# Expert rows scattered to their tokens' places by each block, and read back in order

## The chip, the cores and the metric

The kernel runs on one core of a Trainium2 chip. The metric is the device time of one execution in microseconds. The program in question has three timed runs: 1660.15, 1660.92 and 1669.7 us, with a median of 1660.92. Beside them one execution was recorded by the profiler.

## The reference, cut to what matters

A graph transformer layer over 1250 tokens of width 768 in float32. Two branches (graph attention over 20000 edges, and linear attention) are added to x; then comes a mixture of experts with a shared expert. Only this last part bears on the change:

```python
probs = softmax(x @ router_w)                      # 8 experts
gates, idx = top_k(probs, 2)
gates = gates / sum(gates)
g = silu(einsum('bsd,edh->bseh', x, w_gate))       # each w: [8, 768, 768]
u = einsum('bsd,edh->bseh', x, w_up)
expert_out = einsum('bseh,ehd->bsed', g * u, w_down)
routed = sum over the two chosen experts of gate * expert_out
shared = silu(x @ ws_gate) * (x @ ws_up) @ ws_down # width 384
alpha = sigmoid(x @ sg_w + sg_b)
out = x + alpha * shared + (1 - alpha) * routed
```

In the layer `x` enters this part normalised. Only the two chosen experts of a token have to be computed: 2500 rows of work.

## The kernel before

Tokens are tiled by 125 (`TP`), ten tiles (`NT`). The residual `acc`, 125 x 10 x 768, stays in SBUF for the whole kernel. The program is built with a scheduler that orders each engine's instructions by priority and puts in the waits; a queue (SP, ACT or POOL) issues its DMAs strictly in its own order, each after the semaphores it waits for.

The expert part sorts rows by expert. Each token's two rows get a slot number (`slot`). An expert's slots are rounded up to parts of 64 rows, and two parts make a block of 128 slots. There may be up to 26 blocks (`NBLK`); 22 of them (`NSURE`) run unconditionally, and the last four stand under nested conditions on the number of parts in use (`n_part`).

Five steps matter here.

- **Routing.** Normalised tokens go to DRAM (`xd`, L765). Twenty indirect DMAs on POOL, the puts (L836), write each token's number to `who` at its slot. `who` was zeroed at the start of the kernel, so an unused slot names token 0. SP loads `who` back as `ids` (L842), one column for each block. Meanwhile TensorE computes the shared expert's hidden rows (L880).
- **Inputs of a block.** `gather` (L908) fetches the block's 128 token rows by an indirect DMA on POOL. `fetch` (L915) loads one of the three expert matrices of the block (2304 KB) on SP, into a ring of two places. Since a block can take its first part's weights from either place, a place is loaded again only when the block before has finished with its product.
- **The block.** `rows` transposes the inputs, `gate` and `up` make the hidden rows, `hidden` transposes them, `down` makes the output rows. The loop overlaps `down` of one block with the next block's products. After `down`, VectorE copies the result out of PSUM (L969) and ACT stores it to `ys` in slot order (L970), one plain DMA of 128 x 768.
- **Ahead.** The loop also fetches weights, and gathers rows, for block 22, which stands under a condition; inside the conditions each block does so for the next one.
- **The end.** For each token tile, two indirect DMAs on POOL gather the 125 rows of its two choices from `ys` into `yg` (L1026). For each tile in turn, TensorE multiplies the shared hidden rows by `wsd` (L1034), VectorE adds the shared part (L1037) and the two routed parts (L1039) to `acc`, and the tile is stored, 120 rows by SP (L1042) and 5 by ACT (L1043).

The blocks that do not run leave their `ys` rows unwritten, so four stores of zeros fill them early (L328).

Of the kernel before, what the change touches and what calls it, by code (L numbers as in the profile page):

```python
# [8 lines left out]
F32 = mybir.dt.float32  # L9
# [4 lines left out]
I32 = mybir.dt.int32  # L14
AF = mybir.ActivationFunctionType
ALU = mybir.AluOpType
# [3 lines left out]
P = 128  # L20
TP = 125
NT = 10
N = TP * NT
D = 768
# [21 lines left out]
NBLK = -(-((NE - 2) * NPART - 2 * (-N // PART)) // NPART)  # L46
NSURE = -(-(2 * N + NE * PART // 2) // P)
NSLOT = NBLK * P
# [14 lines left out]
def gps_block(ctx: ExitStack, tc: tile.TileContext, x, src, dst, norm_g, norm_b, W1, a_src1, a_dst1, b1,  # L63
              W2, a_src2, a_dst2, b2, Wu, bu, w_qkv, w_proj, b_proj, router_w, w_gate, w_up, w_down,
              ws_gate, ws_up, ws_down, sg_w, sg_b, out):
    nc = tc.nc
# [2 lines left out]
    big = ctx.enter_context(tc.tile_pool(name="big", bufs=1, reuse_waits="tile"))  # L69
    dram = ctx.enter_context(tc.tile_pool(name="slots", bufs=1, space=bass.MemoryType.DRAM))  # L70

    xd = dram.tile([N, D], F32, name="xd")
    who = dram.tile([NSLOT, 1], I32, name="who")
    ys = dram.tile([NSLOT, D], F32, name="ys")
    xd_t = xd.rearrange("(t p) d -> t p d", p=TP)
    who_b = who.rearrange("(b p) o -> b (p o)", p=P)
    who_p = who.rearrange("(b p) o -> p (b o)", p=P)
    ys_b = ys.rearrange("(b p) d -> b p d", p=P)


    acc = big.tile([TP, NT, D], F32, name="acc")
# [81 lines left out]
    with tc.tile_pool(name="ph1", bufs=1, reuse_waits="tile") as p1, tc.tile_pool(name="ph1w", bufs=2, reuse_waits="tile") as p1w, \  # L163
# [55 lines left out]
        for j in range(2):  # L219
            o = H2 * (C2 + 1) + j * H2  # L220
# [11 lines left out]
        for k in range(KD):  # L232
# [10 lines left out]
            for h in range(H1):  # L243
                o = (h % 2) * CG
# [8 lines left out]
        for h in range(H1):  # L253
            o = (h % 2) * CG
# [20 lines left out]
        for h in range(H2):  # L275
            o = h * (C2 + 1) + C2
# [23 lines left out]
        base = p1.tile([TP, ECH], F32, name="base")  # L300
# [19 lines left out]
    with tc.tile_pool(name="cnt", bufs=1, reuse_waits="tile") as cp, \  # L320
            tc.tile_pool(name="tokps", bufs=2, space=PSUM, reuse_waits="tile") as ps, \
            tc.tile_pool(name="cntps", bufs=3, space=PSUM, reuse_waits="tile") as pcp:

        zero = cp.tile([P, D], F32, name="zero")
        nc.gpsimd.memset(zero, 0.0)
        nc.sync.dma_start(who_b, zero[:NBLK, :P].bitcast(I32))
        for j in range(NSURE, NBLK):
            nc.sync.dma_start(ys_b[j], zero)  # L328

# [66 lines left out]
        for t0 in range(0, NT, 2):  # L398
            ts = range(t0, t0 + 2)
            mv, r, r2 = ahead  # L400
# [210 lines left out]
    with tc.tile_pool(name="h2p", bufs=1, reuse_waits="tile") as hp, tc.tile_pool(name="gatw", bufs=2, reuse_waits="tile") as pw:  # L611
# [23 lines left out]
        with tc.tile_pool(name="wup", bufs=1, side="right", reuse_waits="tile") as wp2, \  # L635
# [53 lines left out]
            o = H2 * (C2 + 1)  # L689
# [19 lines left out]
    fp = ctx.enter_context(tc.tile_pool(name="ffn", bufs=1, reuse_waits="tile"))  # L709

    g2 = fp.tile([TP, NT, 2], F32, name="g2")
    al = fp.tile([TP, NT], F32, name="al")
    slot = fp.tile([TP, 2, NT], I32, name="slot")
    blk = fp.tile([TP, NBLK + 1], I32, name="blk")
    place = fp.tile([TP, NBLK, NPART], I32, name="place")
    ids = fp.tile([P, NBLK], I32, name="ids")
    nh = HS // P
    hTs_s = fp.tile([P, nh, N], F32, name="hTs_s")
    wsd = fp.tile([P, nh, D], F32, name="wsd")
# [13 lines left out]
    with tc.tile_pool(name="fln", bufs=2, reuse_waits="tile") as pw, tc.tile_pool(name="flnps", bufs=1, space=PSUM, reuse_waits="tile") as ps:  # L733
# [8 lines left out]
                                base=0, pattern=[[1, TP]], channel_multiplier=-1)  # L742
# [9 lines left out]
        rev = pw.tile([TP, NT, NE], F32, name="rev", bufs=1)  # L752
        nc.gpsimd.iota(rev, pattern=[[0, NT], [-1, NE]], base=NE, channel_multiplier=0,
                       allow_small_or_imprecise_dtypes=True)
        number = pw.tile([TP, NT], I32, name="number", bufs=1)
        nc.gpsimd.iota(number, pattern=[[TP, NT]], base=0, channel_multiplier=1)
        norms = []
        for t0, n in ((0, 2), (2, 4), (6, 4)):
            mv, r = moments(pw, [acc[:, t, :] for t in range(t0, t0 + n)], f"ln3_{t0}")
# [28 lines left out]
        for r in range(2):  # L788
            m = pw.tile([TP, NT], F32, name=f"r_m{r}", bufs=1)
            nc.vector.tensor_reduce(m, pb, axis=AX.X, op=ALU.max)  # L790
            o = pw.tile(S3, F32, name=f"r_o{r}", bufs=1)
            nc.vector.tensor_tensor(o, pb, m[:, :, None].to_broadcast(S3), ALU.is_equal)
            nc.vector.tensor_mul(o, o, rev)
            f = pw.tile([TP, NT], F32, name=f"r_f{r}", bufs=1)
# [25 lines left out]
        for e in range(NE):  # L820
# [3 lines left out]
                                       op0=ALU.mult, op1=ALU.add)  # L824
# [9 lines left out]
        for t in range(NT):  # L834
            for r in range(2):
                put = nc.gpsimd.indirect_dma_start(  # L836
                    out=who, out_offset=bass.IndirectOffsetOnAxis(ap=slot[:, r, t:t + 1], axis=0),
                    in_=number[:, t:t + 1], in_offset=None, bounds_check=NSLOT - 1, oob_is_err=False)
                for p in puts:
                    tc.declare_no_dep(put.ins, p.ins, reason="slots differ")  # L840
                puts.append(put)
# [49 lines left out]
    with tc.tile_pool(name="fps", bufs=1, space=PSUM, reuse_waits="tile") as ps:  # L891
# [4 lines left out]
        xin = [xpool.tile([P, D], F32, name=f"xin{i}") for i in two]  # L896
# [9 lines left out]
        experts, spots = {}, {}  # L906

        def gather(j):  # L908
            if j < NBLK:
                nc.gpsimd.indirect_dma_start(  # L910
                    out=xin[j % 2], out_offset=None, in_=xd,
                    in_offset=bass.IndirectOffsetOnAxis(ap=ids[:, j:j + 1], axis=0),
                    bounds_check=N - 1, oob_is_err=False)

        def fetch(j, i):  # L915

            if j >= NBLK:
                return
            if i == 0:
                experts[j] = nc.sync.value_load(blk[0:1, j:j + 1], min_val=0, max_val=NE - 1)  # L920
            w = (w_gate, w_up, w_down)[i]
            nc.sync.dma_start(rings[i][:, j % 2], w[bass.ds(experts[j], 1)].rearrange("o (k p) f -> p (o k) f", p=P))

        def places(j):

            at = [j % 2] * NPART
            if j > 0:
                for i in range(NPART - 1):
                    at[i] = nc.tensor.value_load(place[0:1, j, i:i + 1], min_val=0, max_val=1)
            spots[j] = at  # L930
# [20 lines left out]
        def hidden(j):  # L951
            turned(hTs[j % 2], hs[j % 2])

        def gate(j, s):
            h = hs[j % 2][:, s * HALF:(s + 1) * HALF]
            product(j, 0, pgs[s], xTs[j % 2], s)
            nc.scalar.activation(h, pgs[s][:, :HALF], AF.Sigmoid)  # L957
            nc.vector.tensor_mul(h, h, pgs[s][:, :HALF])  # L958
# [6 lines left out]
        def down(j):  # L965
            y = yo[j % 2]
            for s in two:
                product(j, 2, pd[:, s], hTs[j % 2], s)
            nc.vector.tensor_copy(y.rearrange("p (s d) -> p s d", s=2), pd[:, :, :HALF])  # L969
            nc.scalar.dma_start(ys_b[j], y)  # L970


        for j in two:
            gather(j)
            for i in range(2):
                fetch(j, i)
            if j == 0:
                fetch(j, 2)
        places(0)
        rows(0)  # L980
        for j in range(NSURE):
            gate(j, 0)
            if j > 0:
                hidden(j - 1)
            gate(j, 1)
            if j > 0 and j + 1 < NSURE + 1:
                fetch(j + 1, 0)
            if j + 1 < NSURE:
                places(j + 1)
            for s in two:  # L990
                up(j, s)
            if j > 0 and j + 1 < NSURE + 1:
                fetch(j + 1, 1)
            gather(j + 2) if j + 2 < NSURE + 1 else None
            if j + 1 < NSURE:
                rows(j + 1)
            if j > 0:
                down(j - 1)
                fetch(j, 2)
        hidden(NSURE - 1)  # L1000
        down(NSURE - 1)
        fetch(NSURE, 2)

        with ExitStack() as deeper:
            for j in range(NSURE, NBLK):
                deeper.enter_context(tc.If(n_part > j * NPART))
                gather(j + 1)
                places(j)
                rows(j)
                for s in two:  # L1010
                    gate(j, s)
                fetch(j + 1, 0)
                for s in two:
                    up(j, s)
                fetch(j + 1, 1)
                hidden(j)
                down(j)
                fetch(j + 1, 2)
    blocks.close()

    out_t = out.rearrange("(t p) d -> p t d", p=TP)
    with tc.tile_pool(name="comb", bufs=1, reuse_waits="tile") as cb, tc.tile_pool(name="cps", bufs=3, space=PSUM, reuse_waits="tile") as ps:
        ygs = [cb.tile([TP, D], F32, name=f"yg{i}") for i in range(2 * NT)]
        for t in range(NT):
            for r in range(2):
                nc.gpsimd.indirect_dma_start(  # L1026
                    out=ygs[2 * t + r], out_offset=None, in_=ys,
                    in_offset=bass.IndirectOffsetOnAxis(ap=slot[:, r, t:t + 1], axis=0),
                    bounds_check=NSLOT - 1, oob_is_err=False)
        for t in range(NT):  # L1030
            pd = ps.tile([TP, 2, 512], F32, name="pds")
            for s in range(2):
                for f in range(nh):
                    nc.tensor.matmul(pd[:, s, :HALF], hTs_s[:, f, t * TP:(t + 1) * TP],  # L1034
                                     wsd[:, f, s * HALF:(s + 1) * HALF], start=(f == 0), stop=(f == nh - 1))
            av = acc[:, t, :].rearrange("p (s d) -> p s d", s=2)
            nc.vector.scalar_tensor_tensor(av, pd[:, :, :HALF], al[:, t:t + 1], av, op0=ALU.mult, op1=ALU.add)  # L1037
            for r in range(2):
                nc.vector.scalar_tensor_tensor(acc[:, t, :], ygs[2 * t + r], g2[:, t, r:r + 1], acc[:, t, :],  # L1039
                                               op0=ALU.mult, op1=ALU.add)  # L1040

            nc.sync.dma_start(out_t[:TP - 5, t, :], acc[:TP - 5, t, :])  # L1042
            nc.scalar.dma_start(out_t[TP - 5:, t, :], acc[TP - 5:, t, :])  # L1043


# [25 lines left out]
```

## Time and profile before

| What | us |
|---|---|
| median of the three timed runs | 1660.92 |
| the profiled execution | 1667.31 |
| its span, first to last instruction | 1665.6 |
| TensorE busy in it | 1554.5 |
| VectorE busy | 723.7 |
| ScalarE busy | 364.6 |
| GpSimd (POOL) busy | 143.2 |

The page cuts the span into 40 slices, some 41.6 us each, and gives busy shares in tenths. PE is TensorE, DVE is VectorE, ACT is ScalarE. "SPq" and "ACTq" are the queues on which those engines issue DMAs. In a line of the timeline the first number is the start in us from the span's beginning, the second the duration, then the engine, the line of the kernel, the operation and its tiles; the bracket gives the idle time of that engine before it and what ended it. In a row of windows the stretch comes first, then the busy time of each engine with the number of instructions, the granted TensorE clock, the mean busy share of the 16 DMA engines, and GB/s. 22 copies of `y` are in the trace, so the conditional blocks did not run. Routing's first put is at 983.7 us, the first block's products begin at 1039.2, and the last block's end at 1604.8.

### The profile page before, as it was taken

How to read it: one execution, taken by the hardware profiler on the slowest of the kernel's cores; microseconds unless marked ns; L12 is line 12 of the kernel's file. 1: busy time of each engine (PE TensorE's matmuls, PEld its weight loads, DVE VectorE, ACT ScalarE, POOL GpSimd, SP SyncE). 2: the span in 40 equal slices, each digit the busy share in tenths (PEclk: the TensorE clock that was granted, in tenths of full speed). 3: DMA queues.
4: the chain of work that ended last, by engine and by line, in shares of the span. 5: the costliest groups of instructions: out<-in, count | busy, mean ns of one | idle time of the engine just before them, and what ended most of it. 6: DMA issues, size and time to landing. Idle time of an engine off the chain costs nothing. (4 is left out here: it accounts for less than half of the span.)

```text
span 1665.6 us, 18775 instructions
## 1 busy us (share of the span) xinstructions
PE 1554.5 (93%) x7185; PEld 884.8 (53%) x7185; DVE 723.7 (43%) x1337; ACT 364.6 (22%) x623; POOL 143.2 (9%) x174
## 2 busy tenths in 40 slices
PE   5999889998999999999896999999999999999966
PEld 5666544444455599975453864444444444444433
DVE  7888459212444398967788131111111111111106
ACT  3222211111110187840663210111011011011000
POOL 2211000000000000000000123000000000000015
PEclk9999899999999999999998589999999999999988
DMA  6200041002111110020111336888888888888858
GB/s 193 76 1 1 2 140 53 1 0 69 38 38 30 31 56 31 31 73 12 35 44 58 93 57 79 308 315 310 317 312 310 317 313 310 317 314 308 309 173 259
DMA packets 104756, 238.83 MB, mean 143 GB/s; under 512 B 15735, under 2 KB 38391, under 8 KB 104663
## 3 DMA queue, kind: packets, MB, share of 16 engines
q1 hardware_dynamic: 84749, 192.43, 34.5%
q0 software_dynamic: 14544, 35.83, 7.1%
q10 hardware_dynamic: 5370, 9.30, 1.5%
q8 instruction: 63, 1.03, 0.3%
q14 instruction: 30, 0.25, 0.0%
HBM read 219.45 MB, written 18.02 MB: 143 GB/s over the span
## 5 line engine op out<-in xcount | busy, mean ns | idle before, releaser
L939 PE MATMUL pdb<-wd,hT 128*64 128x384 f32 (+1 forms) x1056 | 177.5, 493 | 9.1 <-DMA wd<-in_L_ffn_w_down_dram 9.1
L939 PE MATMUL pgb<-wg,xT 128*64 128x384 f32 (+1 forms) x1056 | 178.8, 489 | 2.2 <-DMA wg<-in_L_ffn_w_gate_dram 1.9
L939 PE MATMUL pub<-wu,xT 128*64 128x384 f32 (+1 forms) x1056 | 174.0, 486 | 0.0
L537 PE MATMUL pp<-wkv,xnT 128*125 128x512 f32 x360 | 161.4, 598 | 0.1
L619 PE MATMUL pa<-G,u 125*125 125x199 f32 x800 | 140.4, 337 | 11.1 <-DVE h L627 6.0
L619 PEld LDWEIGHTS pa<-G,u 125*125 125x125 f32 x800 | 135.6, 190 | 16.2 <-issue 7.2
L939 PEld LDWEIGHTS pdb<-wd,hT 128*64 128x64 f32 x1056 | 75.2, 139 | 100.7 <-issue 97.6
L939 PEld LDWEIGHTS pub<-wu,xT 128*64 128x64 f32 x1056 | 75.9, 137 | 94.3 <-issue 94.3
L939 PEld LDWEIGHTS pgb<-wg,xT 128*64 128x64 f32 x1056 | 74.2, 137 | 92.0 <-issue 90.5
L537 PEld LDWEIGHTS pp<-wkv,xnT 128*125 128x125 f32 x360 | 65.8, 190 | 73.5 <-issue 73.2
L969 DVE COPY y<-pdb 128x768 f32<-128x768 f32 x22 | 21.1, 957 | 189.4 <-PE pdb L939 189.4
L416 PE MATMUL ph<-wg,xnT 128*125 128x400 f32 x240 | 99.3, 519 | 2.8 <-PEq L430 2.7
L600 DVE TENSOR_TENSOR ea<-ea,eb 125x625 f32<-125x625 f32 x120 | 94.0, 804 | 15.6 <-ACT eb L599 7.9
L602 DVE SCALAR_TENSOR_TENSOR u<-ea,cntT 125x625 f32<-125x625 f32 x120 | 94.0, 805 | 14.6 <-PE pa L619 8.0
L958 DVE TENSOR_TENSOR h<-h,pgb 128x384 f32<-128x384 f32 x44 | 24.4, 554 | 173.4 <-ACT h L957 173.4
L599 ACT ACTIVATE eb<-r,g_ss 125x625 f32<-125x625 f32 x120 | 95.1, 816 | 20.6 <-DVE ea L600 20.4
L484 DVE CUSTOM_DVE_ANT_0 junk<-ssb,absent 125x1250 bf16<-125x1250 f32 x60 | 87.7, 1462 | 13.6 <-DMA ssb<-g_srow_d 12.3
L957 ACT ACTIVATE h<-pgb 128x384 f32<-128x384 f32 x44 | 21.6, 491 | 309.2 <-PE pgb L939 309.2
L567 PE MATMUL pq<-xnT,wq 128*128 128x500 f32 (+1 forms) x216 | 82.7, 528 | 4.4 <-DMA wq<-in_L_mix_w_qkv_dram 3.8
L653 PE MATMUL pu<-wu,xnT 128*125 128x384 f32 x240 | 81.7, 490 | 1.4 <-DVE acc L658 1.4
L963 DVE TENSOR_TENSOR h<-h,pub 128x384 f32<-128x384 f32 x44 | 24.4, 554 | 134.4 <-PE pub L939 134.4
L580 PE MATMUL pu<-wp,at 128*125 128x384 f32 x240 | 80.5, 488 | 1.4 <-DVE acc L583 1.0
(240 smaller groups left out, 1765.1 us busy)
## 6 DMA issues: line engine op xcount, KB each, us to landing
wg<-in_L_ffn_w_gate_dram SPq DMA_DIRECT2D x23, 2304.0 KB
wu<-in_L_ffn_w_up_dram SPq DMA_DIRECT2D x23, 2304.0 KB, 9.9
wd<-in_L_ffn_w_down_dram SPq DMA_DIRECT2D x23, 2304.0 KB
ys<-y ACTq DMA_DIRECT2D x22, 384.0 KB, 7.2
r<-g_rrow_d POOLq DMA_DIRECT2D x12, 610.4 KB, 8.3
wq<-in_L_mix_w_qkv_dram SPq DMA_DIRECT2D x18, 384.0 KB, 3.6
wkv<-in_L_mix_w_qkv_dram SPq DMA_DIRECT2D x6, 768.0 KB
acc<-in_x_dram POOLq DMA_DIRECT2D x10, 375.0 KB, 9.6
```

The costliest lines, as they stand in the source:

```text
L416: nc.tensor.matmul(ph[:, :2 * CG], xnT[:, k, tok], wg[:, k, s * 2 * CG:(s + 1) * 2 * CG], start=(k == 0), stop=(k == KD - 1))
L484: nc.vector.tensor_tensor_reduce(out=junk, in0=self.ssb, in1=absent[:, dt, :], scale=1.0, scalar=-3.0e38, op0=ALU.add, op1=ALU.max, accum_ ...
L537: nc.tensor.matmul(pp, xnT[:, k, tok], wkv[:, k, :, :], start=(k == 0), stop=(k == KD - 1))
L567: nc.tensor.matmul(pq[:, :qw], wq[:, k, :], xnT[:, k, tok], start=(k == 0), stop=(k == KD - 1))
L580: nc.tensor.matmul(pu[:, s, :HALF], at[:, k, i * TP:(i + 1) * TP], wp[:, k, s * HALF:(s + 1) * HALF], start=(k == 0), stop=(k == KD - 1))
L599: nc.scalar.activation(eb, r[:, 1, :], AF.Exp, bias=ss02[:, st, h:h + 1])
L600: nc.vector.tensor_max(ea, ea, eb)
L602: nc.vector.scalar_tensor_tensor(u, ea, 1.0, cntT[:, st, half * W:(half + 1) * W], op0=ALU.min, op1=ALU.mult)
L619: nc.tensor.matmul(pa[i][:, :CO + 1], u[:, i * TP:(i + 1) * TP], G[:, st, h, :CO + 1], start=(st == 0), stop=(st == NT - 1))
L653: nc.tensor.matmul(pu[:, :HALF], xnT[:, k, t * TP:(t + 1) * TP], wus[s][:, k, :], start=(k == 0), stop=(k == KD - 1))
L939: nc.tensor.matmul(pt[part, :HALF], rows[:, k, part], w[:, k, s * HALF:(s + 1) * HALF], start=(k == 0), stop=(k == KD - 1))
L958: nc.vector.tensor_mul(h, h, pgs[s][:, :HALF])
```

## The change

Each block writes its rows to where their tokens will look for them. `ys` becomes 2 x 1250 rows: row `r * 1250 + token` holds the row of a token's choice `r`. `who` becomes pairs: the token's number, and its row in `ys`. `number` holds both for both choices. At the start `who` is filled with the pair (0, 2500): an unused slot still gathers token 0, and its row 2500 lies past the bound of the scatter, so it is not written. The zero stores go.

After `down`, POOL scatters the 128 rows by an indirect DMA, in place of ACT's store. At the end SP loads each tile's two choices in one plain DMA, 125 x 2 x 768, in token order. The source asks for the shared parts of three tiles first, and from then on for two routed tiles with each shared one.

Weights and rows are no longer fetched ahead for a block under a condition; such a block does it for itself. In the lead-in, the first block's `down` matrix is fetched after the second block's `gate` and `up`.

```diff
-    who = dram.tile([NSLOT, 1], I32, name="who")
-    ys = dram.tile([NSLOT, D], F32, name="ys")
+    who = dram.tile([NSLOT, 2], I32, name="who")
+    ys = dram.tile([2 * N, D], F32, name="ys")
...
-    who_p = who.rearrange("(b p) o -> p (b o)", p=P)
-    ys_b = ys.rearrange("(b p) d -> b p d", p=P)
+    who_p = who.rearrange("(b p) o -> p b o", p=P)
+    ys_t = ys.rearrange("(r t p) d -> t p r d", r=2, p=TP)
...
-        zero = cp.tile([P, D], F32, name="zero")
-        nc.gpsimd.memset(zero, 0.0)
-        nc.sync.dma_start(who_b, zero[:NBLK, :P].bitcast(I32))
-        for j in range(NSURE, NBLK):
-            nc.sync.dma_start(ys_b[j], zero)
+        nobody = cp.tile([NBLK, P, 2], I32, name="nobody")
+        nc.gpsimd.iota(nobody, pattern=[[0, P], [2 * N, 2]], base=0, channel_multiplier=0)
+        nc.sync.dma_start(who_b, nobody.rearrange("b p o -> b (p o)"))
...
-    ids = fp.tile([P, NBLK], I32, name="ids")
+    ids = fp.tile([P, NBLK, 2], I32, name="ids")
...
-        number = pw.tile([TP, NT], I32, name="number", bufs=1)
-        nc.gpsimd.iota(number, pattern=[[TP, NT]], base=0, channel_multiplier=1)
+        number = pw.tile([TP, 2, NT, 2], I32, name="number", bufs=1)
+        for r in range(2):
+            nc.gpsimd.iota(number[:, r], pattern=[[TP, NT], [r * N, 2]], base=0, channel_multiplier=1)
...
-                    in_=number[:, t:t + 1], in_offset=None, bounds_check=NSLOT - 1, oob_is_err=False)
+                    in_=number[:, r, t, :], in_offset=None, bounds_check=NSLOT - 1, oob_is_err=False)
...
-            nc.scalar.dma_start(ys_b[j], y)
+            nc.gpsimd.indirect_dma_start(
+                out=ys, out_offset=bass.IndirectOffsetOnAxis(ap=ids[:, j, 1:2], axis=0),
+                in_=y, in_offset=None, bounds_check=2 * N - 1, oob_is_err=False)
...
         for j in two:
             gather(j)
             for i in range(2):
                 fetch(j, i)
-            if j == 0:
-                fetch(j, 2)
+        fetch(0, 2)
...
         for j in range(NSURE):
+            more = j + 1 < NSURE
...
-            if j > 0 and j + 1 < NSURE + 1:
+            if j > 0 and more:
                 fetch(j + 1, 0)
...
-            if j > 0 and j + 1 < NSURE + 1:
+            if j > 0 and more:
                 fetch(j + 1, 1)
-            gather(j + 2) if j + 2 < NSURE + 1 else None
+            if j + 2 < NSURE:
+                gather(j + 2)
...
-        fetch(NSURE, 2)
...
-                gather(j + 1)
+                gather(j)
+                for i in range(3):
+                    fetch(j, i)
...
-        ygs = [cb.tile([TP, D], F32, name=f"yg{i}") for i in range(2 * NT)]
+        ygs = [cb.tile([TP, 2, D], F32, name=f"yg{t}") for t in range(NT)]
         for t in range(NT):
-            for r in range(2):
-                nc.gpsimd.indirect_dma_start(
-                    out=ygs[2 * t + r], out_offset=None, in_=ys,
-                    in_offset=bass.IndirectOffsetOnAxis(ap=slot[:, r, t:t + 1], axis=0),
-                    bounds_check=NSLOT - 1, oob_is_err=False)
+            nc.sync.dma_start(ygs[t], ys_t[t])
+
+        def routed(t):
+            for r in range(2):
+                nc.vector.scalar_tensor_tensor(acc[:, t, :], ygs[t][:, r, :], g2[:, t, r:r + 1], acc[:, t, :],
+                                               op0=ALU.mult, op1=ALU.add)
...
+        LATE = 3
         for t in range(NT):
...
+            if t > 2 * LATE:
+                routed(t)
             av = acc[:, t, :].rearrange("p (s d) -> p s d", s=2)
             nc.vector.scalar_tensor_tensor(av, pd[:, :, :HALF], al[:, t:t + 1], av, op0=ALU.mult, op1=ALU.add)
-            for r in range(2):
-                nc.vector.scalar_tensor_tensor(acc[:, t, :], ygs[2 * t + r], g2[:, t, r:r + 1], acc[:, t, :],
-                                               op0=ALU.mult, op1=ALU.add)
...
+            if t > 2 * LATE:
+                store(t)
+            if t >= LATE:
+                for u in range(2 * (t - LATE), 2 * (t - LATE) + 2):
+                    if u <= 2 * LATE:
+                        routed(u)
+                        store(u)
```

More of the change, by code (lines that the diff above doesn't have):

```diff
@@ L908, in gather @@
         def gather(j):
-            if j < NBLK:
-                nc.gpsimd.indirect_dma_start(
-                    out=xin[j % 2], out_offset=None, in_=xd,
-                    in_offset=bass.IndirectOffsetOnAxis(ap=ids[:, j:j + 1], axis=0),
-                    bounds_check=N - 1, oob_is_err=False)
+            nc.gpsimd.indirect_dma_start(
+                out=xin[j % 2], out_offset=None, in_=xd,
+                in_offset=bass.IndirectOffsetOnAxis(ap=ids[:, j, 0:1], axis=0),
+                bounds_check=N - 1, oob_is_err=False)
         def fetch(j, i):
-            if j >= NBLK:
-                return
             if i == 0:
@@ L969, in down @@
             nc.vector.tensor_copy(y.rearrange("p (s d) -> p s d", s=2), pd[:, :, :HALF])
-            nc.scalar.dma_start(ys_b[j], y)
+            nc.gpsimd.indirect_dma_start(
+                out=ys, out_offset=bass.IndirectOffsetOnAxis(ap=ids[:, j, 1:2], axis=0),
+                in_=y, in_offset=None, bounds_check=2 * N - 1, oob_is_err=False)
         for j in two:
@@ L985, in gps_block @@
             gate(j, 1)
-            if j > 0 and j + 1 < NSURE + 1:
+            if j > 0 and more:
                 fetch(j + 1, 0)
-            if j + 1 < NSURE:
+            if more:
                 places(j + 1)
@@ L991, in gps_block @@
                 up(j, s)
-            if j > 0 and j + 1 < NSURE + 1:
+            if j > 0 and more:
                 fetch(j + 1, 1)
-            gather(j + 2) if j + 2 < NSURE + 1 else None
-            if j + 1 < NSURE:
+            if j + 2 < NSURE:
+                gather(j + 2)
+            if more:
                 rows(j + 1)
@@ L1011, in gps_block @@
                     gate(j, s)
-                fetch(j + 1, 0)
                 for s in two:
                     up(j, s)
-                fetch(j + 1, 1)
                 hidden(j)
                 down(j)
-                fetch(j + 1, 2)
     blocks.close()
@@ L1022, in gps_block, with store @@
     with tc.tile_pool(name="comb", bufs=1, reuse_waits="tile") as cb, tc.tile_pool(name="cps", bufs=3, space=PSUM, reuse_waits="tile") as ps:
-        ygs = [cb.tile([TP, D], F32, name=f"yg{i}") for i in range(2 * NT)]
+        ygs = [cb.tile([TP, 2, D], F32, name=f"yg{t}") for t in range(NT)]
         for t in range(NT):
+            nc.sync.dma_start(ygs[t], ys_t[t])
+        def routed(t):
             for r in range(2):
-                nc.gpsimd.indirect_dma_start(
-                    out=ygs[2 * t + r], out_offset=None, in_=ys,
-                    in_offset=bass.IndirectOffsetOnAxis(ap=slot[:, r, t:t + 1], axis=0),
-                    bounds_check=NSLOT - 1, oob_is_err=False)
+                nc.vector.scalar_tensor_tensor(acc[:, t, :], ygs[t][:, r, :], g2[:, t, r:r + 1], acc[:, t, :],
+                                               op0=ALU.mult, op1=ALU.add)
+        def store(t):
+            nc.sync.dma_start(out_t[:TP - 5, t, :], acc[:TP - 5, t, :])
+            nc.scalar.dma_start(out_t[TP - 5:, t, :], acc[TP - 5:, t, :])
+        LATE = 3
         for t in range(NT):
@@ L1035, in gps_block @@
                                      wsd[:, f, s * HALF:(s + 1) * HALF], start=(f == 0), stop=(f == nh - 1))
+            if t > 2 * LATE:
+                routed(t)
             av = acc[:, t, :].rearrange("p (s d) -> p s d", s=2)
             nc.vector.scalar_tensor_tensor(av, pd[:, :, :HALF], al[:, t:t + 1], av, op0=ALU.mult, op1=ALU.add)
-            for r in range(2):
-                nc.vector.scalar_tensor_tensor(acc[:, t, :], ygs[2 * t + r], g2[:, t, r:r + 1], acc[:, t, :],
-                                               op0=ALU.mult, op1=ALU.add)
-            nc.sync.dma_start(out_t[:TP - 5, t, :], acc[:TP - 5, t, :])
-            nc.scalar.dma_start(out_t[TP - 5:, t, :], acc[TP - 5:, t, :])
+            if t > 2 * LATE:
[5 more added lines that the diff above has]
+                        store(u)
 _G, _M, _F = "L0_gnn_", "L0_mix_", "L0_ffn_"
```

## The prediction

> **What bounds the kernel now.** I read the page's busy slices first, then the timeline of the end, then one-microsecond windows of single transfers.
>
> ```profile
> PE   5999889998999999999896999999999999999966
> DMA  6200041002111110020111336888888888888858
> ys<-y ACTq DMA_DIRECT2D x22, 384.0 KB, 7.2
> ```
>
> TensorE is full from start to end; the two exceptions are the drop near 1040 us and the end. In the 22 blocks the DMA engines are about 85% busy, but the blocks repeat every 25.13 us (the gathers of consecutive blocks start at 1502.53 and 1527.67) and TensorE never waits inside them: whatever changes there must first use up slack. So the ends of this stage matter. The last stretch, from the timeline:
>
> ```profile
> 1594.54 10.30 PE L939 MATMUL pdb<-wd,hT 128*64 x48 [9.14 <-DMA wd<-in_L_ffn_w_down_dram]
> ...
> 1604.86 0.37 SPq L922 DMA_DIRECT2D wd<-in_L_ffn_w_down_dram  x1
> ...
> 1605.89 0.33 ACTq L970 DMA_DIRECT2D ys<-y  x1
> ...
> 1616.63 1.28 POOL L1026 DMA_INDIRECT yg<-ys,slot  x1 [87.97 <-SPq L1004]
> ...
> 1651.02 1.68 POOL L1026 DMA_INDIRECT yg<-ys,slot  x1 [0.30 <-issue]
> ...
> 1660.57 1.02 DVE L1039 SCALAR_TENSOR_TENSOR acc<-yg,g,acc 125x768 f32<-125x768 f32 x1 [0.63 <-DMA yg<-ys,slot]
> ```
>
> The last block's matmuls end at 1604.84. Its rows go to DRAM beside an unused 2.3 MB weight load, and POOL gathers only at 1616.63. Twenty gathers are generated one after another until 1652.70, the last lands at 1660.5, and the last store ends the span at 1665.6. From the last matmul to the end: 60.8 us.
>
> **The front of the blocks.** `fetch(1,0)` and `fetch(1,1)` move ahead of `fetch(0,2)` on SP. They depend only on `blk`, so they start about 1030, right behind `ids` (1028.75), not at 1042.5. This removes the one wait for a gate weight, 1.86 us at 1057.53. But the first gathers now share the engines with 4.6 MB of weights: the `xin` gathers land in 3.9 us at best and 7.1 in the median, which is the loop with weights in flight. The first is issued at 1033.76, and TensorE takes it at 1038.02 with no slack, so it would wait up to 7.1-4.3 = 2.8 us. I take 2.8-1.9 = +1; bounds -2 and +3. The `wd` load that falls behind has 30 us (issue 1042, first use 1074.9). `who` pairs are 8 bytes instead of 4, with as many runs: 0, bounded by +4 (a tenth of the 45 us from the first put at 983.73 to `ids`), since the gather behind them has no slack. Three pieces cost nothing: the second iota and the fill of `who` come long before use, and the four dropped zero stores lie before 52 us with idle DMA behind them.
>
> **The blocks.** Each store leaves ACT (0.33 us of issue, not missed) and becomes a POOL scatter. It waits for the copy of y; behind it POOL holds the next gather. In one iteration the gather issues at 1100.40 and y is ready at 1109.05; a scatter, priced by the `xin` gather (1.00 us), ends near 1110.1, and the next gather can start no sooner than 1125.53. Fifteen us of cover, so 0; without it, what the scatter overruns. Each scatter also waits for the one before, landed 15 us earlier. Weights issued about 16 us before use land in about 10, which covers a slower scatter by 6 us. Padding rows are not written, 316 of 2816. So 0; below, nothing is to be had, since TensorE has no wait here to give back; above, 22 us, if each block lost the scatter's microsecond of generation.
>
> The weights no longer fetched for block 22 are 6.9 MB, but TensorE did not wait for them. The last `wd` is issued at 1584.62, only when the earlier down product has ended, and costs 9.14 us of wait either way; the unused `wu` before it landed by 1585.3, before this one's data began. Taken: 0, bounds -1 and 0.
>
> **The end.** Now ten SP loads of 125 x 2 x 768 (768 KB, 7.68 MB together) replace twenty gathers. The same bytes; the question is how many DMA engines move them. Three rows of the windows (columns: window, length, busy time by engine, PE clock, DMA share, GB/s):
>
> ```profile
> 638.00:639.00 1.00, 1.00 (x8) 1.00 (x7) 1.00 (x2) 0.84 (x2) 0.00 (x0) 1.00 0.30 125
> 640.00:641.00 1.00, 0.18 (x1) 0.21 (x2) 1.00 (x5) 0.97 (x2) 0.00 (x0) 1.00 0.30 125
> 947.00:948.00 1.00, 1.00 (x5) 0.71 (x3) 0.00 (x0) 0.09 (x1) 0.00 (x0) 0.50 0.88 184
> 1558.00:1559.00 1.00, 1.00 (x10) 0.46 (x8) 0.00 (x0) 0.00 (x0) 0.00 (x0) 1.00 1.03 409
> ```
>
> At 638 a single `r` load is in flight, 125 x 2 x 625: share 0.30 (five of sixteen is 0.31) and 125 GB/s. At 947 it is a store of 125 whole rows (`xd`), share 0.88; at 1558, 128-row weights at 409 GB/s. Both 125-row cases are issued by POOL. The last store (SP 120 rows, ACT 5 rows) shows the SP and ACT queues:
>
> ```profile
> DMA packets 145, 0.38 MB, mean 94 GB/s; under 512 B 20, under 2 KB 20, under 8 KB 145
> ...
> q1 hardware_dynamic: 135, 0.37, 33.4%
> q10 hardware_dynamic: 10, 0.02, 1.6%
> ```
>
> SP: 120 rows and 15 small packets; ACT: 5 and 5. [...] By the `xd` row the loads would take 7.68 MB at about 300 GB/s, 26 us; by [...]the `r` row 7.68/0.129 (mean of its four full windows, 125 to 135) = 60 us. I take 60: the `r` load has the shape of the new loads, two runs in each of 125 partitions[...]. [...]
>
> The sum, from the last matmul:
>
> - copy of y: 1.0.
> - The scatter, not seen: 3.9 (best gather) to 7.9 (the last put, until `ids`). It moves 128 whole rows, as the gather does: 4.5.
> - Branches and SP's first issue: 0.7, half of the 1.3 us that POOL took at the same place (ys landed 1615.3, gather 1616.63).
> - First packet: 1.0, as the last store shows (share 0.01 until 1662). Loads 60, last landing 0.5.
> - VectorE in the program's built order: the rows of tiles 7, 8 and 9 are asked for between tiles 3 and 6, so nine operations follow the last load: three of L1037 at 1.01 and six of L1039 at 1.02, with gaps 9.3. Behind them queue the stores of tiles 5 to 9.
> - Last store: 4.0 (1661.6 to 1665.6). Stores 0 to 4, held behind the loads on those five engines, drain in 5 us under the 9.3.
>
> 1.0+4.5+0.7+1.0+60+0.5+9.3+4.0 = 81.0, against 60.8: +20.2. The first four terms are the gain: loads may start 7.2 us after the last matmul, where gathers started at 11.8. With the front, +21.2. The profiled execution is 1667.31 us (span 1665.6, 1.7 around it), so it would be 1688.5; it lies 6.4 above the median of 1660.92. On the median: 1682.1.
>
> **Rivals.**
> (1) The loads are spread, on ten or sixteen engines. For: `xd` at 0.88, and the gathers of 125 rows reach 254 GB/s when many are in flight. [...] Loads land every 2.6 us, load 7 near 29; VectorE then sets the end: about 18 of its 30 operations (18.6 us) follow, plus 4 for the store, 52 against 60.8. With the front -8: 1653, not slower. Break-even is loads in 60.8-21-1 = 39 us, 197 GB/s, eight engines at 25.
> (2) The scatters choke the queues. The 20 puts show it: 12.6 us to landing in the median, and the two weight loads beside them stretched. If a scatter held the weights 3 us beyond the 6 us of slack, 22 x 3 = 66: 1748. Against: 128 whole rows, not 125 of 4 bytes.
> (3) The skipped fetch gives back its 22 us: 6.9 MB at 315 GB/s, 1639. Against: no wait on it in the chain, except some 3 us at 1605 to 1616 that the sum holds.
>
> **Numbers.** Five engines 0.83, at 1682, mostly 1674 to 1690 (front and puts -3 to +6, scatter +3, rate 122 to 135 GB/s is -3 to +3); spread loads 0.12; choked scatters 0.04; the fetch's full gain 0.01. Within 1% is what a measurement of this kernel can't tell from no change, here up to 1677.5: about 0.09 of the first case lies there. So slower 0.78, same 0.19, faster 0.03. Leaving out the two small cases and most of rival 1, the range is 1671 to 1694.
>
> **What would show it.** In the windows of the new end, DMA share near 0.31 at 120 to 135 GB/s for some 60 us, VectorE waiting for `yg` 6 us at a time, and nine of its operations after the last landing. Share near 0.8 there is rival 1. The block period stays 25.13 us, and the wait of 9.14 on `wd` stays. Gathers landing later than 8 us, or a wait of TensorE on weights in the middle blocks, is rival 2. I am wrong by sign if SP's queue splits 125 rows otherwise than POOL's `r` load.

## The result, and the profile after

The kernel after takes 1685.4 us in the median of four runs (1681.3 to 1688.0), the kernel before beside it 1662.8 (1660.2 to 1669.7). The ratio is 1.0127, with a 95% interval from 1.0087 to 1.0167: slower, by some 21 us. Its profiled execution took 1688.04 us with a span of 1686.3, against 1667.31 and 1665.6.

From the page of the kernel after: TensorE's and the DMA engines' busy tenths in 40 slices of 42 us, and the row of the new loads.

```profile
PE   6999889999999899998996999999999999999773
DMA  7100041002110100021013155688888888888324
yg<-ys SPq DMA_DIRECT2D x10, 750.0 KB
```

The blocks look as before, full on TensorE and 8 in the DMA row, up to the last one. In the last two slices, where before TensorE stood at 6 and 6 and the DMA engines at 5 and 8, TensorE is at 7 and 3 and the DMA engines at 2 and 4. (The DMA engines' 3 ahead of them is the stretch in which nothing is loaded for block 22 any more.) Here is that end in the timeline, first TensorE's last block, then the other engines (start, length, engine, line, operation; in brackets the idle time before it and what ended that):

```profile
1592.71 9.45 PE L936 MATMUL pdb<-wd,hT 128*64 x48 [9.14 <-SPq L1003]
...
1603.45 0.98 POOL L967 DMA_INDIRECT ys<-y,ids  x1 [18.40 <-DVEq L1003]
1608.13 46.07 SPq L1023 DMA_DIRECT2D yg<-ys  x10
1616.58 2.07 DVE L1027 SCALAR_TENSOR_TENSOR acc<-yg,g,acc 125x768 f32<-125x768 f32 x2 [8.44 <-DMA yg<-ys]
...
1659.15 1.02 DVE L1027 SCALAR_TENSOR_TENSOR acc<-yg,g,acc 125x768 f32<-125x768 f32 x1 [22.22 <-DMA yg<-ys]
...
1671.34 1.95 DVE L1027 SCALAR_TENSOR_TENSOR acc<-yg,g,acc 125x768 f32<-125x768 f32 x2 [1.43 <-DMA yg<-ys]
...
1677.85 1.93 DVE L1046 SCALAR_TENSOR_TENSOR acc<-pds,al,acc 125x768 f32<-125x768 f32 x2
```

The last block's matmuls end at 1602.16. The ten loads run from 1609.2 until the last lands at 1671.3, one every 6.1 us; VectorE waits for them, 22.2 us at a stretch before tile 7, and has nine operations left when the last is in. Windows inside the loads and over the last stores (window, length, busy time by engine, PE clock, DMA share, GB/s):

```profile
1640.00:1641.00 1.00, 0.00 (x0) 0.00 (x0) 0.00 (x0) 0.00 (x0) 0.00 (x0) 0.56 0.32 126
1650.00:1651.00 1.00, 0.00 (x0) 0.00 (x0) 0.00 (x0) 0.00 (x0) 0.00 (x0) 0.50 0.31 123
1679.00:1683.00 4.00, 0.00 (x0) 0.00 (x0) 0.78 (x1) 0.00 (x0) 0.00 (x0) 0.76 0.88 300
```

Five sixteenths of the DMA engines at 123 to 126 GB/s while every other engine is idle: the loads alone set the time. The same queue's 120-row stores reach 300 GB/s a moment later. In the packet records each of the loads comes with five packets of 4 bytes, each of these stores with fifteen, and each 128-row weight load, at a share of 1.03 in the prediction's row, with sixteen. Five, fifteen and sixteen engines are my estimates from these counts and the shares.

### The profile page after: what moved, and what is told of

It is laid out like the page before. It is cut to its first block, busy times and chain, and to the rows that moved or that the text cites. A ratio compares the mean times of both kernels' runs of the same rounds, so it can differ in the third digit from the quotient of the medians.

```text
span 1686.3 us, 18775 instructions
## 1 busy us (share of the span) xinstructions
PE 1555.1 (92%) x7185; PEld 882.3 (52%) x7185; DVE 722.3 (43%) x1337; ACT 364.6 (22%) x623; POOL 135.0 (8%) x176
## 3 DMA queue, kind: packets, MB, share of 16 engines
q8 instruction: 63, 1.03, 0.2%
## 4 chain that ended last, share of the span: by engine, by line
issue 30%; PE 30%; DVE 11%; DMA 10%; ACT 3%; POOL 3%; SPq 1%; POOLq 0%; DVEq 0%; ACTq 0%
PE pp L536 6%; PE pu L579 5%; PE pq L566 5%; DVE junk L483 4%; DMA ys<-y,ids 4%; PE pa L618 4%; DMA yg<-ys 3%; DVE ea L599 2%; PE pn L668 2%; ACT eb L598 2%; PE pn L571 1%; PE pu L652 1%; ACT ea L596 1%; PE pl L773 1%; PE pm L681 1%
## 6 DMA issues: line engine op xcount, KB each, us to landing
acc<-in_x_dram POOLq DMA_DIRECT2D x10, 375.0 KB, 10.4
```

## The experiments

Theory: the row count 125 holds the loads to five of the sixteen DMA engines (share 0.31 to 0.33); the rest of the loss is VectorE's order. Rivals: the queue or the rows are slow on any number of engines; or the parts that go with the change (the skipped weights, the pairs) have costs or gains of their own. A ratio is always to the kernel before on the same chip; the brackets behind it are its 95% interval.

**Other engines for the loads.** First, 120 rows on SP and five on ACT:

```diff
-            nc.sync.dma_start(ygs[t], ys_t[t])
+            nc.sync.dma_start(ygs[t][:120], ys_t[t][:120])
+            nc.scalar.dma_start(ygs[t][120:], ys_t[t][120:])
```

> Each tile's load is cut into 120 rows on SP and 5 rows on ACT; nothing else differs from the changed kernel. Five engines: [...] the SP part runs on 15 engines, 7.37 MB at about 25.8 GB/s each is 19 us (21 with the 5-row parts on five of them) where the ten loads took 62; VectorE's 18 operations behind load 7 then set the end. DMA share near 0.9 while the loads run; 35 us off, about 1650 us, below the kernel before. Rival, the loads are slow because they read rows that were just scattered, or because SP issues them one behind the other: share stays near 0.32, time stays at 1685.

Measured: 1667.6 us, ratio 0.9998 [0.9979, 1.0018]: the whole loss is gone, with the same bytes, all but a twenty-fifth of them on the same queue. But it stops short of what I had expected. Its windows and timeline:

```profile
1616.00:1620.00 4.00, 4.00 (x14) 2.30 (x13) 2.87 (x3) 0.00 (x0) 0.00 (x0) 1.00 0.99 206
1620.00:1624.00 4.00, 3.99 (x13) 2.03 (x11) 2.15 (x3) 0.00 (x0) 0.00 (x0) 1.00 0.97 213
```

```profile
1644.28 1.02 DVE L1028 SCALAR_TENSOR_TENSOR acc<-yg,g,acc 125x768 f32<-125x768 f32 x1 [12.08 <-DMA yg<-ys]
```

The engines are full (share 0.97 to 0.99), yet move only 206 to 213 GB/s. In the trace's packet records a packet of 3072 bytes takes 231 ns in the median, where on five engines it takes 122. The loads last 35 us, not 20. That became the second question below.

The other direction, 124 rows on SP and one on ACT (the same edit with 124):

> Each tile's load is cut into 124 rows on SP and 1 row on ACT. Five engines: [...] with fewer bytes on SP (7.62 MB) the loads get slower: share 0.25 at 103 GB/s, 74 us instead of 62, about 1697 us. Rival, it is the bytes, the queue or the reading of scattered rows, not the row count: no change from 1685; or some odd remainder of 125 rows is handled apart, and 124 is faster.

Measured: 1704.2 us, ratio 1.0219 [1.0175, 1.0263]. One row fewer in a load makes the kernel slower by another 15 us. The share is 0.26, four sixteenths:

```profile
1620.00:1624.00 4.00, 2.08 (x7) 0.92 (x5) 0.00 (x0) 0.00 (x0) 0.00 (x0) 1.00 0.26 84
```

Beside the one-row loads of the first 15 us packets are slower than later (71 and 84 GB/s in two windows from 1616 on, at the same share, against some 100 by a load of 744 KB every 7.6 us); over the whole stretch the median is still 122 ns. From the third tile on a load lands every 7.6 us instead of 6.1, five fourths, and the last one 83 us after the first packet instead of 62. So the share goes with the row count and not with the bytes: 0.26 with 124 rows, 0.31 to 0.33 with 125, 0.97 to 0.99 with 120 and the five beside them. The engine counts 4, 5 and 15 divide 124, 125 and 120; whether that decides them is not shown. Third, the whole loads issued by POOL:

```diff
-            nc.sync.dma_start(ygs[t], ys_t[t])
+            nc.gpsimd.dma_start(ygs[t], ys_t[t])
```

> The ten loads of 125 x 2 x 768 are issued by POOL instead of SP, whole. [...] with several loads in flight they lie on different engines, as two r loads did (share 0.6), so the rate climbs to 250 GB/s or more, 30 us for the loads, about 1655 us. Rival, five engines and the same five from POOL too: share 0.31 to 0.33, about 1685.

Measured: 1674.6 us, ratio 1.0042 [1.0020, 1.0063]. POOL does spread 125 rows over all sixteen engines, but again at a share of 1.01 to 1.06 for 192 to 208 GB/s (1616 to 1624):

```profile
1616.00:1620.00 4.00, 1.12 (x2) 0.82 (x3) 3.31 (x4) 0.00 (x0) 1.16 (x1) 0.63 1.01 208
```

It is the same signature as with 120 rows, from another queue and without five-row loads of ACT beside it.

**VectorE's order.** The 125-row loads as built, but each tile's shared operation, two routed ones and store in turn:

```diff
-            if t > 2 * LATE:
-                routed(t)
             nc.vector.scalar_tensor_tensor(av, pd[:, :, :HALF], al[:, t:t + 1], av, op0=ALU.mult, op1=ALU.add)
-            if t > 2 * LATE:
-                store(t)
-            if t >= LATE:
...
+            routed(t)
+            store(t)
```

> The loads as in the changed kernel; VectorE takes the tiles strictly in order (shared part, two routed parts, store), as the kernel before did. The nine operations behind the last load become three, 5.5 us less, and one store instead of four remains at the end, 2.5 us less: about 1677 us, if the last landing sets what follows. Rival, the stores' shares on the five loaded engines set the end: they still drain behind the loads, and the time stays within 2 us of 1685.

Measured: 1682.0 us, ratio 1.0091 [1.0062, 1.0120], 6 us better than the kernel after, where 8 were expected. The two intervals overlap, so the times alone do not show it; in the traces the stretch from the last matmul to the end is 80.9 us instead of 84.1. Only two operations follow the last load, at 1667.80:

```profile
1667.80 2.07 DVE L1027 SCALAR_TENSOR_TENSOR acc<-yg,g,acc 125x768 f32<-125x768 f32 x2 [2.93 <-DMA yg<-ys]
```

Both edits together, 120 rows and this order:

> Both edits at once: 120 rows on SP and 5 on ACT, and VectorE in strict order of the tiles. If the two costs are separate (five engines, and nine operations with five tiles' stores held behind the last load), the order gives about what it gave alone, 6 us: some 1661, ratio to the kernel before about 0.996. With it, 11.5 MB of loads and stores at about 240 GB/s need 48 us from 1610, which gives the same end. If the bytes alone set the end of the 120-row kernel, the order changes nothing: about 1667, ratio 1.000.

Measured: 1661.9 us, ratio 0.9953 [0.9934, 0.9972]. The order gives some 7 us here, and the intervals with and without it do not overlap: the two costs are separate, and the bytes alone did not set the end of the 120-row kernel.

**The parts that go with it.** The kernel before with nothing loaded for the conditional block (its core; the gather of that block goes too, and the conditional code fetches for itself):

```diff
-            if j > 0 and j + 1 < NSURE + 1:
+            if j > 0 and j + 1 < NSURE:
                 fetch(j + 1, 0)
...
-        fetch(NSURE, 2)
```

> The kernel before, with only the weights and rows for the conditional block left out and the first down weights fetched after the others (as in the kernel after); rows are stored and gathered as before. My step: no gain in the blocks, and 1.86 us at the most where the first gate weight was waited for: ratio 0.998 to 1.001. The rival, that the skipped 6.9 MB are time given back: 22 us less, ratio 0.987.

Measured: 1663.5 us, ratio 0.9964 [0.9943, 0.9985]: a gain of some 6 us (2 to 10), not 22, but more than I gave it. Two places in its timeline, the first block and the first gather of the end:

```profile
1042.53 1.51 PE L945 MATMUL ptr<-ident,xin 128*128 128x128 f32 x6 [4.10 <-DMA xin<-xd,ids]
...
1600.02 10.30 PE L939 MATMUL pdb<-wd,hT 128*64 x48 [9.23 <-DMA wd<-in_L_ffn_w_down_dram]
1615.55 1.28 POOL L1023 DMA_INDIRECT yg<-ys,slot  x1 [106.62 <-SPq L1002]
```

At the front it loses: `wg(1)` and `wu(1)`, issued at 1031.75 and 1033.61, now move beside the first gather, which is issued at 1035.4 and lands in some 7.1 us (7.0 to 7.2); TensorE waits 4.1 us for it, and that front is 5 us longer in all. The wait of 9.2 on the last `wd` stays. At the end it gains: the first gather comes 5.2 us after the last matmul (1610.32) instead of 11.8, since no unused 2.4 MB lie ahead of the last rows; from the last matmul to the end it is 53.9 us, not 60.8. The net in these two profiled executions is small, 1664.2 against 1665.6 us of span.

The kernel before with the slot list as pairs of 8 bytes, and nothing else (`number` and `ids` follow):

```diff
-    who = dram.tile([NSLOT, 1], I32, name="who")
+    who = dram.tile([NSLOT, 2], I32, name="who")
...
-                    in_=number[:, t:t + 1], in_offset=None, bounds_check=NSLOT - 1, oob_is_err=False)
+                    in_=number[:, r, t, :], in_offset=None, bounds_check=NSLOT - 1, oob_is_err=False)
```

> The kernel before, with only the slots' records made pairs of 8 bytes instead of single 4-byte numbers. If it is the pairs that let the puts land in 8.5 us instead of 12.6, they do so here, the list is read some 8 us or more sooner, and the first gathered rows land before TensorE asks for them: ratio about 0.998. If what landed sooner in the kernel after was due to the other edits of the front (no zero stores, order of the first weights), the puts land in about 12.6 us here and the ratio is 1.000.

Measured: 1664.1 us, ratio 0.9984 [0.9969, 1.0000]: 2.7 us, just at the edge of what the runs resolve; the trace says it more plainly. The list's tile in the kernel before (what POOL waited for, and the landing of the puts), then with pairs alone, then after:

```profile
L842 SPq DMA_DIRECT2D ids<-who x1: 371/371/371, 1028.8 to 1028.8; - x1
...
  POOL who L836: 9.5, 4
...
DMA to landing us min/median/max: 5.5/12.6/20.0
```

```profile
L843 SPq DMA_DIRECT2D ids<-who x1: 371/371/371, 1013.2 to 1013.2; - x1
```

```profile
L842 SPq DMA_DIRECT2D ids<-who x1: 372/372/372, 1015.4 to 1015.4; - x1
...
DMA to landing us min/median/max: 2.8/8.5/9.8
```

With pairs alone the list is read 15 us sooner (some 13 counted from the first put, as in the kernel after), and POOL no longer stalls between puts. The wait of 1.86 us for block 1's gate weight is gone too, with pairs alone and then in the kernel after:

```profile
1053.80 4.09 PE L940 MATMUL pgb<-wg,xT 128*64 x24 [0.24 <-ACT xT L947]
```

```profile
1055.70 4.09 PE L936 MATMUL pgb<-wg,xT 128*64 x24 [0.24 <-ACT xT L943]
```

It is the pairs.

Both together, which is the change without the new way of the routed rows:

> Everything of the change except the way of the routed rows: pairs of 8 bytes in the list, nothing loaded for the conditional block, first weights in the new order; rows are stored in slot order and gathered as before. The profiles gave 2 us in the front by the pairs, and 6.9 us at the end where no unused weights lie ahead of the last rows; the first gathered rows, which came 4 us late in the kernel without the pairs, are early with them. Together 9 us: about 1658, ratio 0.9945. If the pairs don't mend the late first gather: 4 us, ratio 0.9975. The scattered rows with their loads would then cost 30 us, or 25, against these parts.

Measured: 1654.1 us, ratio 0.9914 [0.9885, 0.9944], 14 us (9 to 19); the 9 expected lie at the edge. Its profile shows the two gains: no wait for the first gather, and POOL's first gather 6.2 us after the last matmul (1600.43):

```profile
1606.59 1.28 POOL L1024 DMA_INDIRECT yg<-ys,slot  x1 [107.20 <-PE pds L1032]
```

So by the times the rest of the change is worth 14 us, and the scattered rows with their ordered loads, as built, cost 1.0127/0.9914 = 1.0215, 35 us (27 to 44 with both intervals). The traces show less of both. Of the 10.4 us by which this profiled span is shorter than the one before, 2.4 lie ahead of the first put (981.3 instead of 983.7); some 8 are left for the rest of the change. From the last matmul to the end it is 54.8 us here and 84.1 in the kernel after: 29 us for the new way of the rows.

**Why fifteen engines move only 210 GB/s.** The 120-row loads again, from an input instead of the scattered rows:

```diff
-    ys_t = ys.rearrange("(r t p) d -> t p r d", r=2, p=TP)
+    ys_t = w_down.rearrange("e h d -> (e h) d")[:2 * N].rearrange("(r t p) d -> t p r d", r=2, p=TP)
```

> The 120-row kernel with the loads at the end taking as many rows of the same form, 120 partitions with two runs each, 3.84 MB apart, from an input (the down weights) instead of the scattered rows; the routed rows are so left out of the sum. With five engines a packet of 3072 bytes took 122 ns, with fifteen 231 ns. If it is the source (the kernel's own DRAM space) that holds fifteen engines at 215 GB/s, packets take about 122 ns here and the loads some 20 us. If it is the form of the transfer, or the number of engines with it, packets stay near 230 ns and 215 GB/s.

Measured, in its one execution: packets of 201 ns in the median instead of 231. The source matters by an eighth; it is not the cause. One run in each partition instead of two:

```diff
-            nc.sync.dma_start(ygs[t][:120], ys_t[t][:120])
+            for r in range(2):
+                nc.sync.dma_start(ygs[t][:120, r, :], ys_t[t][:120, r, :])
```

> The 120-row kernel in tile order, with each of its ten SP loads (two runs of 3072 bytes in a partition, 3.84 MB apart) split in two loads of one run each, as the kernel loads x at its start, where fifteen engines moved 400 GB/s at 121 ns a packet. If the two distant runs make packets take 231 ns, they take about 121 here: loads in some 21 us, VectorE's thirty operations then set the end, some 1645 to 1650, ratio 0.988. If fifteen engines reading such rows are held to 215 GB/s in any form, nothing changes: about 0.995, as with two runs.

Measured: 1658.2 us, ratio 0.9944 [0.9923, 0.9965], like two runs; packets 206 ns. A premise of that expectation was false: the 121 ns packets at the kernel's start are weights of 128 partitions; `x` comes there by POOL, 125 rows at a time, in packets of 6144 bytes at 367 ns in the median, so about as slowly as the loads here (184 ns for 3072 bytes). Then four large loads, five runs in a partition as far apart as those of the weights:

```diff
+        for t0 in (0, 5):
+            for r in range(2):
+                yg = cb.tile([TP, 5, D], F32, name=f"yg{t0}_{r}")
+                nc.sync.dma_start(yg[:120], ys_r[r][:120, t0:t0 + 5])
+                nc.scalar.dma_start(yg[120:], ys_r[r][120:, t0:t0 + 5])
```

> The 120-row kernel in tile order, with four large SP loads (120 partitions with five runs each, 384 KB apart, one choice and five tiles at a time) instead of ten: the form of the expert weights (128 partitions, six runs 393 KB apart), which move at 409 GB/s. If the form decides, packets take about 121 ns, the loads some 21 us, and the first tile is whole after about 11 us: end some 1648, ratio 0.990. If the rows are held to 215 GB/s in any form, the first tile comes only after about 18 us and VectorE runs behind: about 1668, ratio 1.000.

Measured: 1671.7 us, ratio 1.0025 [1.0010, 1.0040]; 174 to 200 GB/s at a share of 1.0 (1616 to 1624), packets near 245 ns, and VectorE waits 17.4 us for the first tile. The form is not the cause either. What all slow loads still had in common was 120 or 125 partitions. So 128:

```diff
+        ys_n = ys.rearrange("(r n) d -> n r d", r=2)
+        ygs = [cb.tile([P, 2, D], F32, name=f"yg{t}") for t in range(NT)]
+        for t in range(NT - 1):
+            nc.sync.dma_start(ygs[t], ys_n[t * TP:t * TP + P])
...
-                nc.vector.scalar_tensor_tensor(acc[:, t, :], ygs[t][:, r, :], g2[:, t, r:r + 1], acc[:, t, :],
+                nc.vector.scalar_tensor_tensor(acc[:, t, :], ygs[t][:TP, r, :], g2[:, t, r:r + 1], acc[:, t, :],
```

> Tile order, with nine of the ten loads taking 128 rows of each choice on SP instead of 120 and 5; the three rows too many, which belong to the next tile, are not used. In the traces every load or gather of 120 or 125 rows of the scattered rows, on ten to sixteen engines, ran at 190 to 255 GB/s in all, from two sources and in three forms, and only loads of 128 partitions (the weights) ran at 409 GB/s with 121 ns a packet. If the 128 partitions make the difference, packets take about 121 ns here, the nine loads some 18 us, and VectorE's thirty operations set the end: some 1645 to 1650, ratio 0.988. If it is something else about these rows, packets stay at 200 to 235 ns, with 2% more bytes: about 1660, ratio 0.995, and the cause stays open.

Measured: 1651.9 us, ratio 0.9913 [0.9885, 0.9940]. The windows, and VectorE in the timeline:

```profile
1616.00:1620.00 4.00, 4.00 (x14) 2.30 (x13) 3.89 (x5) 0.00 (x0) 0.00 (x0) 1.00 1.03 403
1620.00:1624.00 4.00, 4.00 (x14) 2.38 (x13) 3.93 (x5) 0.00 (x0) 0.00 (x0) 1.00 1.03 400
```

```profile
1612.64 2.07 DVE L1030 SCALAR_TENSOR_TENSOR acc<-yg,g,acc 125x768 f32<-125x768 f32 x2 [4.70 <-DMA yg<-ys]
...
1634.02 1.02 DVE L1047 SCALAR_TENSOR_TENSOR acc<-pds,al,acc 125x768 f32<-125x768 f32 x1 [0.74 <-PE pds L1044]
1635.07 2.07 DVE L1030 SCALAR_TENSOR_TENSOR acc<-yg,g,acc 125x768 f32<-125x768 f32 x2
```

400 GB/s at 121 to 126 ns a packet, from the same rows and by the same queue, with eight more partitions in a load (and, by the share of 1.03, sixteen engines instead of fifteen). VectorE waits once for rows (4.7 us) and later only for TensorE, whose shared product (`pds`) now sets the end. The one load left at 120 rows still shows packets of 211 ns, though its five ACT rows had landed long before: those small loads are not the cause. This version beats both kernels. By the times it can't be told from the change without the new way of the rows (0.9914), so most of its gain on the kernel before is that of the other parts. From the last matmul to the end its trace shows 47.2 us, that of the other 54.8; whether the scatter with such loads is really better than the gathers stays open.

## Why the prediction was right, and where its steps were not

**Direction and size** held: +20.7 us between the two profiled spans, where the sum said +21.2; 1685 where it said 1682. Two of its terms missed in opposite directions, the front 3.5 us too high and the end 3.1 too low, so that the sum came this close is partly luck.

- **Front, +1: wrong in sign.** From the end of the shared gate and up products (1038.13 before, 1038.00 after) to the last matmul it is 566.7 us before and 564.2 after: -2.5. Of this, 1.7 lie ahead of the first down product: the wait for the gate weight, taken off rightly, though the pairs alone remove it too. The other 0.8 is the last down product itself, 9.45 us instead of 10.30, for which no run gives a reason. The 2.8 of the late first gather never came. The step that failed is "`who` pairs are 8 bytes instead of 4, with as many runs: 0, bounded by +4". The pairs brought the list some 13 us sooner, and with it the first gather (1020.30 instead of 1033.76), so that its landing no longer mattered. The step beside it, that the gather sharing the engines with the weights makes TensorE wait up to 2.8, is right where the list comes late: 4.1 in the kernel without the pairs.
- **Blocks, 0: right.** The gathers still follow each other by 25.13 us; the scatters take 1.03 us on POOL and land in 2.9 to 8.8 us (7.2 in the median), within the 15 us of cover. The wait of 9.14 on the last `wd` is there to the digit. Rival 2, choked queues, is refuted.
- **Skipped weights, 0: right in place, small in size.** Nothing came back inside the blocks. The gain sits behind the last matmul, where the prediction had it inside its first terms (loads after 7.2 us, gathers after 11.8: 4.6). Without them the gathers of the kernel before start 6.6 us sooner, and 5.6 with the pairs as well. Rival 3's 22 us are refuted.
- **The five engines, 60 us for the loads: right.** That an SP load of 125 rows moves like POOL's `r` load was an estimate. Measured: 62.1 with the landing (60.5 predicted), share 0.31 to 0.33 at 123 to 135 GB/s, and with 124 rows a share of 0.26.
- **The end's other terms**, predicted and measured: copy 1.0 and 1.0; scatter 4.5 and 3.2; branches and SP 0.7 and 1.8; first packet 1.0 and 1.1; nine operations 9.3 and 8.4; last store 4.0 and 6.5. The last store is the largest miss: four tiles' stores come within 2 us and drain together (share 0.92 to 0.95 from 1678 to 1682), where before only the last one was left (0.30 in the last 5.1 us). SP's earlier stores, issued from 1654.3 behind the loads, move from 1660 on, by the GB/s of the windows about 1 MB of them by 1666. In all 84.1, not 81.0.
- **Rival 1, spread loads, was mispriced.** It put them at 26 us and the kernel at 1653. On fifteen engines they take 35 us and the kernel is level with before. A sign of it stands in the prediction's own rows: the 125-row `xd` store made 184 GB/s at a share of 0.88, the weights 409 at 1.03. Only 128 partitions, with VectorE's order changed as well, reach what the rival assumed: 1652.

## What to carry to other kernels

Before moving a stream onto SP, measure the DMA share that its row count gives: here 124, 125, 120 and 128 rows gave 0.26, 0.31 to 0.33, 0.97 to 0.99 and 1.03, and loads of 83, 62, 35 and about 20 us. A full share at half the rate, as the 206 to 213 GB/s of the 120-row loads against 400 to 403, is a sign too: see whether the fast transfers of the same profile have 128 partitions, and load the extra rows if they cost nothing. And cut a bundle of edits: what was named first in this change cost some 30 us as built, while its small print gained some 10.

## What the runs showed of the hardware

**Loads of less than 128 partitions on many engines.** In the median, a 3072-byte packet takes 122 ns on four or five engines, with 124 or 125 partitions; on fifteen, with 120 partitions, 201 to 245 in three forms and from two sources; on sixteen, with 128 partitions, 121 to 126. Two SP loads of 96 partitions earlier in the kernel before, `wub` at 10.4 and 733.4 us, come with sixteen packets of 4 bytes each, and their packets of 3072 bytes take 213 and 194 ns; the first moves 254 GB/s at a share of 1.07 (14.8 to 16.3). Stores of the same 120 rows take 121 ns. But fewer than 128 partitions are not always slow: the 125-row gathers of the kernel before come mostly in packets of 6144 bytes that take 234 ns in the median, 318 in the mean, so a row takes 117 and 159. Why a 120-row load takes up to twice 121 ns a packet stays open: no run here shows which engine writes which partition, and the gathers show that the number of partitions alone does not decide.

**Indirect scatters of 4 and of 8 bytes.** The same twenty puts land in 12.6 us in the median with 4 bytes a row and in 8.5 with 8. Why twice the bytes land sooner stays open.
